# Two more attention units normalised and projected on the chip instead of through DRAM

## The chip, the cores and the metric

The kernel runs on one core of one Trainium2 chip. The metric is the device time of one execution in microseconds (us); lower is better. Times of views of the profile count from the start of the profiled span.

## The reference, cut to what matters

Two residual blocks on x of shape (4, 1024, 256), that is B = 4 sequences of T = 1024 tokens with C = 256 channels, all in float32:

```python
# block 1: causal attention along T, 16 heads of 16 channels, ALiBi bias
qkv = layernorm(x) @ w_attn.T
att = softmax(q @ k.T / 4 + bias)          # per head, keys up to the query
x   = x + (att @ v) @ w_proj.T
# block 2: an encoder layer on layernorm(x): attention among the B = 4 rows at
# each position, layer norm, then one of 8 experts (two linear layers with a
# GELU between) for each token, layer norm; added to x
x   = x + encoder_layer(layernorm(x))
```

The part that the change touches is the end of block 1: dividing `att @ v` by the sums of the softmax (normalising), and multiplying by `w_proj` (projecting) before the sum goes into x.

## The kernel before, in words

**Blocks and units.** T is cut into 8 column blocks of 128 queries. Attention is computed in 20 *units* (list `units`, indices 0 to 19). Units 0 to 11 take one sequence and two column blocks. The last two column blocks, the seventh and the eighth, are taken one at a time: units 12 to 15 are the four sequences of the seventh block, units 16 to 19 the four sequences of the eighth. Unit 15 is "the seventh block's fourth unit", unit 18 "the last unit but one", unit 19 is `last_unit`.

**Positions.** Each unit treats its 16 heads in G = 4 groups of four heads, g0 to g3. The keys of a group are taken in *rounds* of up to 512 columns. Two rounds make one *position* of the main loop; a late unit has two rounds a group, so one position a group. `begins[u]` is the first position of unit u. In this text (18 g2) is the position of unit 18, group 2. A position issues, in this order: the score matmuls `sk` of its first round (`score_next`; TensorE into PSUM, then `exp` on ScalarE into tiles `p`, then a causal mask on GpSimd), an "E slot" (VectorE work), a "D slot" (TensorE work of other stages), the `sk` of its second round, and the matmuls `pv` (probabilities times values, `weigh_next`) of the position before. After `pv`, ScalarE or VectorE moves the result to a tile `yt`. Row 16 of each head's 32 rows in `yt` is the sum of the softmax.

**PSUM.** During attention PSUM is four pairs of banks, `s0` to `s3`, given out strictly in turn (`pair_of_banks`). A round of scores takes two pairs, a `pv` takes one, and work in the D slot takes halves of further pairs (`bank`, which hands out the second half of the last pair first). Whoever asks for a pair waits until the readers of its last contents have finished.

**Way through DRAM (units 0 to 18).** `weigh` stores `yt` to DRAM (`y`). Some us later the planner issues `load_sums` (sums from DRAM, laid out over partitions), `invert` (reciprocal on VectorE, stored to DRAM as `r`), `load_y` (two broadcast loads `su` of `r`, two loads `yc` of y), `divide` (`yc` times `su`, VectorE) and `project` (four rows of matmul `op`, with `wp`, then VectorE adds PSUM to x in `add_attended`). The due times after the unit's last `pv` are the constants `SUMS_BY` to `PROJECTED_BY` (7, 14, 18, 29 and 31 us by the planner's clock).

**Way on the chip (unit 19 alone).** `normalise(g)` multiplies `yt` by the constant matrix `slot_sum` on TensorE, which spreads each head's sum over its 32 rows (`sum`), takes the reciprocal of the 128x128 result on VectorE and multiplies it with `yt` (`yn`). `project_slots` multiplies the four `yn` with `wp_slots`, a copy of `w_proj` in the 32-row layout that `load_slotted` fetches.

**What follows.** Once all four sequences of column block i are in x, a `front(i)` is queued: layer norm, projection `qkvp`, attention among the four rows (`pr`, `sc`, `pv` and `ctx` on VectorE), output projection `ao`, layer norm, routing (`key`, `best`, `hot`, `rank`, `place`). At most two fronts run together, and `E` stages go to VectorE while `D` stages go to a D slot. The fronts share the single tile `qkv`, so one front's `qkvp` copies wait until the front before has read it for the last time. When attention ends, the tail starts: front(7), what is left of front(6), and then the 38 tiles of the experts.

**Order.** All engines run in the order in which this program issues instructions (`manual_schedule`). The order comes from a planner that keeps a clock for TensorE, VectorE and ScalarE (`time`), adds an estimated cost for each step (for a D slot's work, VectorE is charged 0.35 of the stated cost), and takes a stage once its estimated inputs are ready. So a change of one unit's steps also moves other steps from one position to another. Every instruction issued through `Core` has the source line L587; the names of tiles tell the groups apart.

Of the kernel before, what the change touches and what calls it, by code (L numbers as in the profile page):

```python
# [29 lines left out]
F32 = mybir.dt.float32  # L30
# [7 lines left out]
P = 128  # L38
B, T, C = 4, 1024, 256
H, D, E = 16, 16, 8  # L40
S = 32
G = H // 4
NT = T // P
# [3 lines left out]
W = 256  # L47
PC = W // P
NC = T // W
# [22 lines left out]
KQ_BUFS = 2  # L72
# [3 lines left out]
SUMS_BY, INVERTED_BY, Y_BY, DIVIDED_BY, PROJECTED_BY = 7.0, 14.0, 18.0, 29.0, 31.0  # L76
# [529 lines left out]
def fast_layer(ctx: ExitStack, tc: tile.TileContext, odd, x, wq, wk, wv, wp, w_in, w_out, w_r,  # L606
# [32 lines left out]
    fact = ctx.enter_context(pool("fact", 1))  # L639
    ends = ctx.enter_context(pool("ends", 1))  # L640
# [3 lines left out]
    act = attention.enter_context(pool("act", 1))  # L644
# [16 lines left out]
    def pair_of_banks(name):  # L661
        half_of.clear()
        n_pairs[0] += 1
        taken.append(n_pairs[0] % 4)
        return ps_s.tile([P, 2, QC], F32, tag=f"s{n_pairs[0] % 4}", name=name)

    def bank(name):
        if tail_banks:
            return tail_banks[0].tile([P, QC], F32, tag="m", name=name)
        if half_of:  # L670
            return half_of.pop()
        pair = pair_of_banks(name)
        halves[pair.tensor.name] = [], []
        half_of.append(pair[:, 1])
        return pair[:, 0]

    batches = [(c, b) for c in range(NC) for b in range(B)]
# [2 lines left out]
    units = [(n, 0, PC if n < (NC - 1) * B else 1) for n in range(NC * B)]  # L680
    units += [(n, i, 1) for i in range(1, PC) for n in range((NC - 1) * B, NC * B)]
    last_unit = len(units) - 1
    xs = {}

    def load_x(n):
# [161 lines left out]
    sums, at = [], 0  # L847
# [4 lines left out]
    held = {}  # L852
# [187 lines left out]
    def heads_of(n):  # L1040
        return y_of[n].rearrange("g p w -> (g p) w").rearrange("(h s) w -> h s w", s=S)

    def load_sums(u):
        part_of_row = units[u][2] * H
        nc.sync.dma_start(
            sums[u], heads_of(u)[:, D].rearrange("h (k w) -> h k w", w=part_of_row)
        )
# [30 lines left out]
    def add_attended(u, pm):  # L1078
        n, i, size = units[u]
        at = xs[batches[n]][:, i:i + size].rearrange("p n c -> p (n c)")  # L1080
        nc.vector.tensor_tensor(at, at, pm[:, :size * C], ALU.add)

    def project(u):
        yc, _ = held.pop(("y", u))
        pm = bank(f"op_{u}")
        for i in range(units[u][2]):
            for cc in range(CC):
                nc.tensor.matmul(
                    pm[:, i * C:(i + 1) * C], yc[:, cc, i * P:(i + 1) * P], wp_sb[:, cc],
                    start=cc == 0, stop=cc == CC - 1,  # L1090
                )
        add_attended(u, pm)
# [4 lines left out]
    for j in range(4):  # L1097
        at = slice(j * S, (j + 1) * S)
# [11 lines left out]
                )  # L1110
            held["wp"].append(w)

    def normalise(g):
        if g % 2 == 0:
            held["yn", g // 2] = ends.tile([P, 2, W], F32, tag="su", name=f"yn_{g}", bufs=2)
        yt, yn = (held[k, g // 2][:, g % 2, :P] for k in ("yt", "yn"))
        pm = bank(f"sum_{g}")[:, :P]
        nc.tensor.matmul(pm, slot_sum, yt, start=True, stop=True)
        nc.vector.reciprocal(yn, pm)
        nc.vector.tensor_tensor(yn, yn, yt, ALU.mult)  # L1120

    def project_slots():
        pm = bank(f"op_{last_unit}")
        for g in range(G):
            nc.tensor.matmul(
                pm[:, :C], held["yn", g // 2][:, g % 2, :P], held["wp"][g // 2][:, g % 2],
                start=g == 0, stop=g == G - 1,
            )
        add_attended(last_unit, pm)


    def numbered(name, shape, pattern, up=0, base=0, dtype=F32, into=keep):
# [878 lines left out]
    queue, running = [], []  # L2011
# [78 lines left out]
    begins = [0]  # L2090
# [4 lines left out]
    def at_E(k, what, cost=0.0):  # L2095
        of_E.setdefault(k, []).append((cost, what))

    def at_D(k, cost, what):
        of_D.setdefault(k, []).append((cost, what))
# [4 lines left out]
    for u, (n, i, size) in enumerate(units):  # L2104
        c, b = batches[n]
# [17 lines left out]
    due_E, due_D = [], []  # L2123

    def attended(u, at):
        size = units[u][2]
        if u == last_unit:
            return
        for by, what, cost in (
            (SUMS_BY, load_sums, 0.0), (INVERTED_BY, invert, 0.3), (Y_BY, load_y, 0.0),  # L2130
            (DIVIDED_BY, divide, 0.5),
        ):
            due_E.append((at + by, cost, lambda what=what: what(u)))
        due_D.append((at + PROJECTED_BY, 0.9 * size, lambda: projected(u)))

    def projected(u):
        n, i, size = units[u]
        c, b = batches[n]
        project(u)
        if b == B - 1:  # L2140
            queue.extend(front(PC * c + i + k, fact, 1, False) for k in range(size))

    def pop_due(due, now):
        some = sorted((it for it in due if it[0] <= now), key=lambda it: it[0])
# [1 line left out]
            due.remove(it)  # L2146
        return [(cost, what) for _, cost, what in some]

    at_E(2 * begins[last_unit] + 1, load_slotted)
    for g in range(2):  # L2150
        at_D(begins[last_unit] + 2 + g, 0.5, lambda g=g: normalise(g))

    def more_rows():
        nc.vector.tensor_scalar(q_by, q_by, -4.0, at_row, ALU.mult, ALU.add)
# [74 lines left out]
    def weigh_next(some):  # L2229
        taken.clear()  # L2230
        weigh(some)
        end = on_tensor(SWITCH + sum(columns_of(u, r) for u, _, r, _ in some) * COLUMN)
        read_at(busy("ACT", 0.4, end))
        u, g, r, _ = some[-1]
        if g == G - 1 and r == n_rounds(u) - 1:
            attended(u, time["ACT"])
# [27 lines left out]
    for it in running:  # L2264
        it.ready = 0.0
    for g in range(2, G):
        normalise(g)
    load_sums(last_unit)
    project_slots()
    tail = ctx.enter_context(pool("tail", 1))  # L2270
    work = ctx.enter_context(pool("work", 2))
    ps_x = ctx.enter_context(pool("ps_x", 1, space=PSUM))
# [53 lines left out]
    def begin(it):  # L2326
        if it.kind == "DQ" and ("qkv",) in held or it.kind[1:] == "C" and part.placed < NT - 1:
            return 1e9
        return max(it.ready, free[engine_of[it.kind[0]]])
# [26 lines left out]
    while threads:  # L2356
# [4 lines left out]
        at, _, it = min((begin(it) + FIRST_BY * n, n, it) for n, it in enumerate(threads))  # L2361
# [14 lines left out]
    n = 0  # L2376
    while experts.left():
# [4 lines left out]
        if n == 11:  # L2382
            pm = bank("n_badp")
# [4 lines left out]
@with_exitstack  # L2388
def tile_layer(ctx: ExitStack, tc: tile.TileContext, *args):
    nc = tc.nc  # L2390
    flag = ctx.enter_context(tc.tile_pool(name="flag", bufs=1))
    odd = flag.tile([P, 1], I32, tag="odd", name="odd")
    fast_layer(tc, odd, *args)
    again = nc.values_load(
        odd[0:1, 0:1], min_val=0, max_val=1,
        skip_runtime_bounds_check_because="a comparison's result",
    )
    with tc.If(again > 0):
        general_layer(tc, *args)
# [75 lines left out]
```

## Time and profile before

| | |
|---|---|
| three runs | 836.48, 839.2, 842.09 us; median 839.2 us |
| the profiled execution | 839.28 us, of which the span is 837.1 us |
| mean granted TensorE clock | 0.94 |
| busy over the span | TensorE 719.4 us (86%), VectorE 544.6 us (65%), ScalarE 416.6 us (50%), GpSimd 251.1 us (30%) |
| last `pv` of attention starts | 628.07 us |
| last sum of attention into x (unit 19, `x<-op`) | 641.60 us |

The profiled execution lies on the median, 0.08 us from it. The busy shares are means over three stages with different limits: attention up to some 630 us, the two last fronts up to some 700 us, and the experts. In a timeline of one engine each line has the start, the duration, the engine, line and operation, the tiles (out<-in), the shape, the count and, in brackets, the idle time before with the engine and tile that ended it.

### The profile page before, as it was taken

How to read it: one execution, taken by the hardware profiler on the slowest of the kernel's cores; microseconds unless marked ns; L12 is line 12 of the kernel's file. 1: busy time of each engine (PE TensorE's matmuls, PEld its weight loads, DVE VectorE, ACT ScalarE, POOL GpSimd, SP SyncE). 2: the span in 40 equal slices, each digit the busy share in tenths (PEclk: the TensorE clock that was granted, in tenths of full speed). 3: DMA queues.
4: the chain of work that ended last, by engine and by line, in shares of the span. 5: the costliest groups of instructions: out<-in, count | busy, mean ns of one | idle time of the engine just before them, and what ended most of it. 6: DMA issues, size and time to landing. Idle time of an engine off the chain costs nothing. (4 is left out here: it accounts for less than half of the span.)

```text
span 837.1 us, 22503 instructions
## 1 busy us (share of the span) xinstructions
PE 719.4 (86%) x8917; PEld 540.2 (65%) x8917; DVE 544.6 (65%) x1316; ACT 416.6 (50%) x625; POOL 251.1 (30%) x360
## 2 busy tenths in 40 slices
PE   4988879995999999998989999999983689678982
PEld 2766657674666756665667767787762368567772
DVE  7337224546678877946964739487695869884663
ACT  1455436563647556735654658578460235323540
POOL 5534102211113221102211212122130235637885
PEclk9799889998999999998999999999997699978997
DMA  7454444424344324333354635445315512333430
GB/s 215 117 148 137 143 134 134 144 63 123 94 119 129 108 77 147 98 104 95 93 142 141 185 109 144 123 126 158 94 53 195 177 37 90 93 97 120 124 103 24
DMA packets 75219, 99.56 MB, mean 119 GB/s; under 512 B 19496, under 2 KB 58723, under 8 KB 74596
## 3 DMA queue, kind: packets, MB, share of 16 engines
q1 hardware_dynamic: 64576, 79.63, 32.1%
q0 software_dynamic: 4864, 14.16, 5.6%
q10 hardware_dynamic: 5668, 4.25, 1.7%
q8 instruction: 73, 1.20, 0.6%
q14 instruction: 38, 0.31, 0.1%
HBM read 61.55 MB, written 35.12 MB: 115 GB/s over the span
## 5 line engine op out<-in xcount | busy, mean ns | idle before, releaser
L587 ACT ACTIVATE p<-sk 128x1024 f32<-128x1024 f32 (+1 forms) x320 | 287.0, 939 | 162.8 <-PE sk L587 147.8
L986 POOL TENSOR_SCALAR_AFFINE_SELECT p<-p 128x512 f32<-128x512 f32 (+1 forms) x160 | 103.6, 651 | 397.8 <-ACT p L587 395.9
L587 PE MATMUL sk<-slots 32*128 32x128 f32 (+1 forms) x3456 | 181.7, 328 | 21.2 <-DVE kq L587 10.0
L587 PEld LDWEIGHTS sk<-slots 32*128 32x128 f32 x3456 | 138.1, 188 | 64.9 <-issue 26.8
L587 PE MATMUL pv<-p,v 128*32 128x128 f32 (+1 forms) x3456 | 144.5, 314 | 10.4 <-ACT p L587 4.6
L587 PEld LDWEIGHTS pv<-p,v 128*32 128x32 f32 x3456 | 96.7, 111 | 48.3 <-issue 8.3
L587 PE MATMUL qkvp<-w_in,ut 128*128 128x264 f32 (+1 forms) x224 | 79.1, 489 | 0.0
L587 PEld LDWEIGHTS qkvp<-w_in,ut 128*128 128x128 f32 x224 | 40.3, 194 | 26.7 <-issue 22.4
L587 PE MATMUL oe<-w,ge 128*128 (+1 forms) x152 | 45.2, 423 | 12.9 <-DVE given L587 4.5
L587 PE MATMUL qkp<-xt,wqk 128*128 128x256 f32 x208 | 54.4, 407 | 0.2 <-ACT p L587 0.2
L1813 POOL DMA_INDIRECT given<-rows,rows x38 | 43.2, 1137 | 27.6 <-DVE at_t L587 11.6
L587 PE MATMUL hid<-mt,w 128*128 128x128 f32 x304 | 47.0, 293 | 0.5 <-ACT ge L587 0.5
L587 PEld LDWEIGHTS qkp<-xt,wqk 128*128 128x128 f32 x208 | 39.6, 200 | 11.1 <-issue 3.3
L587 ACT COPY qkv<-qkvp 128x512 f32<-128x512 f32 (+1 forms) x28 | 15.3, 555 | 58.5 <-PE qkvp L587 43.9
L587 PEld LDWEIGHTS hid<-mt,w 128*128 128x128 f32 x304 | 41.9, 200 | 2.0 <-ACT ge L587 1.0
L587 DVE COPY qkv<-qkvp 128x264 f32<-128x264 f32 x28 | 11.9, 431 | 46.9 <-PE qkvp L587 46.8
L1929 POOL DMA_INDIRECT out_dram<-o,out_rows x38 | 38.9, 1024 | 8.8 <-issue 6.3
L587 DVE TENSOR_REDUCE sc<-pr 128x64 f32<-128x1024 f32 x32 | 39.0, 1220 | 1.1
L587 PEld LDWEIGHTS oe<-w,ge 128*128 128x128 f32 x152 | 28.0, 205 | 17.8 <-DVE given L587 5.7
L587 DVE TENSOR_TENSOR pv<-qkv,sc 128x1024 f32<-128x1024 f32 x32 | 39.2, 1224 | 0.4 <-issue 0.3
L587 DVE TENSOR_TENSOR pr<-qkv 128x1024 f32<-128x1024 f32 x32 | 39.2, 1226 | 0.0
L587 PE MATMUL vp<-wv,xt 128*128 128x256 f32 x128 | 35.3, 423 | 0.0
(333 smaller groups left out, 1040.2 us busy)
## 6 DMA issues: line engine op xcount, KB each, us to landing
slots<-k SPq DMA_DIRECT2D x128, 80.0 KB
k<-kq SPq DMA_DIRECT2D x32, 256.0 KB
v<-v SPq DMA_DIRECT2D x16, 288.0 KB
v<-v SPq DMA_DIRECT2D x4, 1152.0 KB
x<-in_x_dram SPq DMA_DIRECT2D x16, 256.0 KB
y<-yt SPq DMA_DIRECT2D x16, 256.0 KB
rows<-x SPq DMA_DIRECT2D x32, 128.0 KB
slots<-k SPq DMA_DIRECT2D x64, 64.0 KB
```

What stands on the lines that cost most here:

```text
L587: ins = made(*args, **kwargs)
L986: nc.gpsimd.affine_select(blocks, blocks, pattern=[[0, 2], [0, size], [1, P]], compare_op=ALU.is_ge, fill=0.0, base=0, channel_multiplier=-1,)
L1813: nc.gpsimd.indirect_dma_start(out=self.hx, out_offset=None, in_=t.rows_of, in_offset=bass.IndirectOffsetOnAxis(ap=t.rows_[:, self.j:self. ...
L1929: ins = nc.gpsimd.indirect_dma_start(out=out.rearrange("t n c -> (t n) c"), out_offset=bass.IndirectOffsetOnAxis(ap=t.table.out_rows[:, t. ...
```

## The change

Unit 15 and unit 18 go the way that unit 19 goes. Step by step:

- `on_chip = (15, 18, 19)`. For 15 and 18, `attended` issues only `load_sums` (the sums are still wanted for a later check), and no `invert`, `load_y`, `divide` or `project`.
- For each of the two, `normalise(u, g)` is put into the D slots of positions `begins[u] + 2 + g`, g = 0 to 3, and `project_slots(u)` into that of `begins[u] + 6`. The next unit begins at `begins[u] + 4`, so the last two sums and the projection stand in the positions g0 to g2 of the following unit.
- `load_slotted` moves from the start of unit 19 to the start of unit 14.
- The tiles `yn` of units 15 and 18 are taken from the buffers of `kq`, the second `yn` tile of unit 19 from those of `yc`.
- A front is queued when all four of its units are projected, counted in `n_projected`, and no longer by the index of the sequence.

```diff
+    on_chip = ((NC * B - 1), last_unit - 1, last_unit)
...
-    def normalise(g):
+    def normalise(u, g):
         if g % 2 == 0:
-            held["yn", g // 2] = ends.tile([P, 2, W], F32, tag="su", name=f"yn_{g}", bufs=2)
-        yt, yn = (held[k, g // 2][:, g % 2, :P] for k in ("yt", "yn"))
-        pm = bank(f"sum_{g}")[:, :P]
+            held["yn", u, g // 2] = (
+                ends.tile([P, 2, W], F32, tag="yc" if g else "su", name=f"yn_{u}_{g}", bufs=2)
+                if u == last_unit else
+                act.tile([P, 2, W], F32, tag=f"kq{g // 2}", name=f"yn_{u}_{g}", bufs=KQ_BUFS)
+            )
+        yt, yn = (held[k][:, g % 2, :P] for k in (("yt", g // 2), ("yn", u, g // 2)))
+        pm = bank(f"sum_{u}_{g}")[:, :P]
         nc.tensor.matmul(pm, slot_sum, yt, start=True, stop=True)
         nc.vector.reciprocal(yn, pm)
         nc.vector.tensor_tensor(yn, yn, yt, ALU.mult)
 
-    def project_slots():
-        pm = bank(f"op_{last_unit}")
+    def project_slots(u):
+        pm = bank(f"op_{u}")
         for g in range(G):
             nc.tensor.matmul(
-                pm[:, :C], held["yn", g // 2][:, g % 2, :P], held["wp"][g // 2][:, g % 2],
+                pm[:, :C], held["yn", u, g // 2][:, g % 2, :P], held["wp"][g // 2][:, g % 2],
                 start=g == 0, stop=g == G - 1,
             )
-        add_attended(last_unit, pm)
+        add_attended(u, pm)
...
     def attended(u, at):
         size = units[u][2]
-        if u == last_unit:
+        if u in on_chip:
+            if u < last_unit:
+                due_E.append((at + SUMS_BY, 0.0, lambda: load_sums(u)))
             return
...
+    n_projected = [0] * NT
+
     def projected(u):
         n, i, size = units[u]
-        c, b = batches[n]
-        project(u)
-        if b == B - 1:
-            queue.extend(front(PC * c + i + k, fact, 1, False) for k in range(size))
+        c = batches[n][0]
+        (project_slots if u in on_chip else project)(u)
+        for k in range(PC * c + i, PC * c + i + size):
+            n_projected[k] += 1
+            if n_projected[k] == B:
+                queue.append(front(k, fact, 1, False))
...
-    at_E(2 * begins[last_unit] + 1, load_slotted)
-    for g in range(2):
-        at_D(begins[last_unit] + 2 + g, 0.5, lambda g=g: normalise(g))
+    at_E(2 * begins[on_chip[0] - 1], load_slotted)
+    for u in on_chip:
+        for g in range(2 if u == last_unit else G):
+            at_D(begins[u] + 2 + g, 0.5, lambda u=u, g=g: normalise(u, g))
+        if u < last_unit:
+            at_D(begins[u] + 2 + G, 1.8, lambda u=u: projected(u))
...
     for g in range(2, G):
-        normalise(g)
+        normalise(last_unit, g)
     load_sums(last_unit)
-    project_slots()
+    project_slots(last_unit)
```

## The prediction

> **What bounds the kernel now.** I read the page first, then the table by stages around the end of attention, then the timelines of VectorE and TensorE there.
>
> The page's busy line says TensorE over the whole span, which hides that the stages differ:
>
> ```profile
> PE 719.4 (86%) x8917; PEld 540.2 (65%) x8917; DVE 544.6 (65%) x1316; ACT 416.6 (50%) x625; POOL 251.1 (30%) x360
> ```
>
> By stages (columns: stretch, length, busy us and instructions of PE, PEld, DVE, ACT, POOL, granted clock, DMA share, GB/s):
>
> ```profile
> 520.00:560.00 40.00, 39.72 (x752) 30.73 (x752) 26.30 (x55) 24.32 (x33) 7.84 (x13) 1.00 0.38 111
> 560.00:590.00 30.00, 27.79 (x690) 23.84 (x690) 22.45 (x49) 23.02 (x29) 6.01 (x11) 1.00 0.57 163
> 590.00:630.00 40.00, 35.97 (x726) 27.52 (x718) 31.41 (x73) 21.06 (x27) 9.62 (x13) 1.00 0.21 62
> 630.00:642.00 12.00, 5.77 (x20) 4.43 (x16) 3.60 (x8) 0.27 (x1) 0.00 (x0) 0.72 0.66 221
> 642.00:665.00 23.00, 9.08 (x45) 4.88 (x45) 21.83 (x61) 4.11 (x8) 5.49 (x5) 0.69 0.48 160
> ```
>
> The reader should see three limits in turn. To 590, TensorE is full. From 630 to 642 nothing is: VectorE 3.60 and TensorE 5.77 of 12 us. From 642 to 665 VectorE is full, 21.83 of 23. VectorE's timeline names the hole:
>
> ```profile
> 629.12 0.25 DVE L587 RECIPROCAL inverse<-sums 128x16 f32<-128x16 f32 x1
> 635.29 0.43 DVE L587 TENSOR_TENSOR yc<-yc,su 128x256 f32<-128x256 f32 x1 [5.92 <-DMA yc<-y]
> 637.97 0.42 DVE L587 TENSOR_TENSOR x<-x,op 128x256 f32<-128x256 f32 x1 [2.25 <-PE op L587]
> 638.33 0.96 DVE L587 RECIPROCAL yn<-sum 128x128 f32<-128x128 f32 x1
> 641.60 0.42 DVE L587 TENSOR_TENSOR x<-x,op 128x256 f32<-128x256 f32 x1 [0.79 <-PE op L587]
> 641.94 0.35 DVE L587 TENSOR_TENSOR own<-low_con,expert 128x192 f32<-128x192 f32 x1
> ```
>
> Unit 18 goes through DRAM after attention has ended; unit 19's last sums stand behind it on TensorE and VectorE. I take the start of `own`, 641.94, as the mark: from there VectorE has no gap to 665, and the order of instructions from there on is the same in the changed program on PE, DVE and ACT. Whatever moves `own` moves the end.
>
> For attention's price per position I use the starts of `pv`:
>
> ```profile
> 547.39 1.96 PE L587 MATMUL pv<-p,v 128*32 128x128 f32 x64
> 551.62 1.95 PE L587 MATMUL pv<-p,v 128*32 128x128 f32 x64 [0.28 <-ACT p L587]
> 554.61 1.13 PE L587 MATMUL op<-wp,yc 128*128 128x256 f32 x4
> 556.94 1.95 PE L587 MATMUL pv<-p,v 128*32 128x128 f32 x64
> ...
> 617.95 1.95 PE L587 MATMUL pv<-p,v 128*32 128x128 f32 x64
> 620.93 0.49 PE L587 MATMUL sum<-yt,slot_sum 128*128 128x128 f32 x2
> 623.26 1.96 PE L587 MATMUL pv<-p,v 128*32 128x128 f32 x64
> 628.07 1.96 PE L587 MATMUL pv<-p,v 128*32 128x128 f32 x64 [2.85 <-DVE count L587]
> ```
>
> A position with an empty D slot takes 4.23 us (547.39 to 551.62); with one `op`, 5.32; with one `sum` (next instruction 0.33 later), also 5.31. So I price a D slot at 1.09 us or its TensorE time, whichever is more. The last line matters most: the last `pv` waits 2.85 us for a bank that VectorE, late, has yet to read (`count`).
>
> **What the Trainium skill says.** "PSUM — Partial Sum Buffer", section "Engine vs sequencer instructions": VectorE's queue is strictly first in, first out, and matmuls start in program order. The trace agrees: unit 19's `sum` and `yn` stand behind unit 18's wait. [...] Here `inverse` at 629.12 needs a store and a load in series before `yc` at 635.29, 6.2 us for both with their issue[...]. "VectorE: DVE Perf Modes", section "First, the fixed hardware budget": the reciprocal is an iterated divide. The trace agrees: 951 ns for `yn<-sum` 128x128 against 292 for the product of that size.
>
> **Removed after attention.** Unit 18's waits and steps, 629.12 to 638.33 on VectorE. The next limit is the last `yt` copy (ends 630.36) and its `sum`; with these at 631, unit 19's last sums would end with `own` at about 634.6. Taken alone: 641.94 - 634.6 = 7.3 us gained. Per unit three VectorE pieces (0.25 + 0.43, the sum into x stays) and five DMAs on SP's queue go too. I cost SP at 0: nothing waited on it there except `yc`.
>
> **Added on TensorE in attention**, in positions from the instruction order of the changed program:
> - Unit 15: three `sum` alone in empty slots, (15 g2), (15 g3), (16 g0): unit 15, with 7 key blocks, pays 0.91 for a small D slot (`pv` at 500.37, 505.29 and 509.30: 4.92 with one `op`, 4.01 empty), so 0.91 + 0.91 + 1.0 = 2.8. The fourth beside `qkvp`: 0.32. Projection has 8 matmul passes for 4: `op` of unit 15 costs 2.0 at (16 g2), and 1.09 goes at (17 g1). `op` of unit 14 moves from (16 g3) to (16 g2): 0. Sum +4.0.
> - Unit 18 up to the end of the D slot of (19 g0): `sum` and `utp` join `ctp` at (18 g2), 2.36 for 1.09, +1.27. At (18 g3) `sum`, `op` of unit 16, `ao` and one `qkvp`, 8.1 for 4.94, +3.16. At (19 g0) 8.48 for 9.08, -0.6. Sum +3.8. The last `qkvp` of front(6), before at (19 g1), is now in (19 g0).
> - Waits for banks held by a late VectorE, found by walking both queues: the first `sum` of unit 15 comes at 508.4 but VectorE is in `pr`/`sc` to 511.2 (0.9 us); `rank` (0.3 more than its 0.73 now); `utp` behind `u` (0.6). Sum +1.8, an estimate from below 0 to 4: a different interleaving may lose nothing.
>
> The D slot of (19 g0) ended at 602.98; now at 602.98 + 4.0 + 3.8 + 1.8 = 612.6.
>
> **Added on VectorE, where I think it decides.** Eight `yn` pairs of 1.26 us (616.98 to 618.24) = 10.1, less 2 x 0.68. The planner charged 0.18 each, so it does not see the delay. In the changed order, all this stands behind the last `qkv` copy, which now waits for TensorE at 612.6 + 0.6 = 613.2 (spacings measured in the old timeline): `u` 1.30, `key` 0.78, `yc` 0.35, `best` to `equal` 1.45, told 0.15, `equal` to `hot` 2.37, `yn` 1.26, `x` 0.35, `u<-rows` 2.40, `pr`/`sc` 2.39, `x` 0.36, `yn` 1.26, `rank` to `at_place` 3.36, three `pr`/`sc` 7.2, `yn` 1.26. Sum 26.2, so `count` comes at 639.4 against 627.86. TensorE wants that bank at about 633.6 (its 625.2, + 4.0 + 1.8, and + 2.3 for unit 18 with (19 g1) 2.94 shorter and (19 g2) 1.44 longer, plus 0.3): it waits some 6 us instead of 2.85. Last `pv` 639.6 to 641.6, `sum` to 641.8, first `yn` at 642.1, and from `yn` to `own` 3.6 us as now (638.33 to 641.94): `own` at 645.7. That is 3.8 us later; with 0.2 us for the pieces I rounded, 4.0.
>
> Covered at nothing: the earlier `load_slotted` (two GpSimd memsets of 0.5 us, 8 DMAs of 0.45 us on SP) lies beside GpSimd's idle time and ahead of slot fills needed a unit later; if not covered, up to 3.6 us. The experts' weights, issued at 634.10 now, start some 9 us later, but their first copy is at 693.23.
>
> Sum on the profiled execution: 839.28 + 4.0 = 843.3 us; it lies on the median, so that is the forecast for it too, +0.5%. A measurement here tells about 1% from no change.
>
> **Rivals.**
> A. *The removed wait wins.* If VectorE does the 26.2 us list in under 20, TensorE decides the end: last `pv` at 633.6, `own` at 639.7, -2.2 us, 837; without the bank waits (1.8) and with lone sums at their own 0.32 (2.0), 833. All of the 7.3 would be 832. For it: VectorE idles some 15 us between 585 and 613 waiting for `qkvp`. Against: its order puts the list behind those copies.
> B. *Slower by over 1%: banks pinned by VectorE.* Eight `sum` banks are each freed only by a reciprocal queued behind front work; a wait of one `pr` and `sc` (2.4 us) at three of them beyond the 1.8 above gives +7.2, 850. It decides from two such waits, 848. For: VectorE is busy 18.29 of 20 us at 500 to 520. Against: TensorE comes back to the same pair only some 3.5 us later.
> C. *Nothing moves*: the 4.0 and errors of the walk cancel, 839. Counted in the forecast's own range.
>
> **How the numbers follow.** Forecast with C (838 to 847.7): 0.52. A: 0.28, of which 0.12 under 830.9 (gains in the order that I don't see). B: 0.20. So faster by over 1% 0.12, within 1% 0.68, slower 0.20. The range 831 to 851 leaves out A's far part (0.12) and that of B (some 0.08).
>
> **What would show it.** Right: `inverse` and its 5.92 us gone after 629; the last `pv` waits about 6 us for `count` near 639; `own` near 646; `pv` periods with a lone `sum` near 5.3. Wrong: no wait for `count` and `own` before 640 (A), or waits of `sk` or `pv` for `yn` over 1 us in units 15 to 19 (B). A changed duration from 642 on in the tail would break the mark.

## The result, and the profile after

The changed kernel takes 841.5 us (median of 20 executions, 838.26 to 846.82), beside 836.4 us for the kernel before on the same chip (833.48 to 843.03): ratio 1.0055, 95% interval 1.0037 to 1.0073. It is 0.55% slower, and the interval leaves out 1. The profiled execution took 843.85 us, its span is 842.1 us, the mean granted clock 0.94. In the traces the end of attention, from the last `pv` to unit 19's sum into x, became 6.2 us shorter, and 12 to 13 us were paid before it (the table by cuts below).

The busy line of the page:

```profile
PE 722.7 (86%) x8941; PEld 542.8 (64%) x8941; DVE 552.2 (66%) x1328; ACT 416.9 (49%) x625; POOL 253.4 (30%) x360
```

The table by stages (stretch, length, busy us and instructions of PE, PEld, DVE, ACT, POOL, granted clock, DMA share, GB/s):

```profile
590.00:630.00 40.00, 36.14 (x577) 27.27 (x581) 25.85 (x70) 18.78 (x24) 4.87 (x9) 1.00 0.22 62
630.00:642.00 12.00, 6.69 (x167) 5.75 (x164) 10.75 (x14) 4.20 (x6) 3.00 (x3) 0.88 0.05 13
642.00:665.00 23.00, 12.17 (x87) 7.05 (x79) 19.13 (x55) 3.93 (x8) 4.89 (x5) 0.77 0.56 191
```

Where no engine was full before (630 to 642, VectorE 3.60 us), VectorE is now full with 10.75 of 12 us. In 590 to 630 it is less busy than before (31.41 us): its work has moved back. VectorE's timeline shows what it is full of:

```profile
613.04 0.43 DVE L587 COPY qkv<-qkvp 128x264 f32<-128x264 f32 x1 [2.29 <-PE qkvp L587]
...
637.34 1.22 DVE L587 TENSOR_REDUCE sc<-pr 128x64 f32<-128x1024 f32 x1
638.48 0.95 DVE L587 RECIPROCAL yn<-sum 128x128 f32<-128x128 f32 x1
639.53 0.29 DVE L587 TENSOR_TENSOR yn<-yn,yt 128x128 f32<-128x128 f32 x1
639.74 0.16 DVE L587 TENSOR_SCALAR count<-sum 128x8 f32<-128x8 f32 x1
...
647.31 0.42 DVE L587 TENSOR_TENSOR x<-x,op 128x256 f32<-128x256 f32 x1 [0.79 <-PE op L587]
647.65 0.35 DVE L587 TENSOR_TENSOR own<-low_con,expert 128x192 f32<-128x192 f32 x1
```

From the last `qkv` copy to `count` VectorE works for 26.7 us without a wait. TensorE's timeline shows who waits for that, and two waits earlier on:

```profile
592.48 1.13 PE L587 MATMUL sum<-wp,yc 128*128 128x256 f32 x4 [2.17 <-DVE yc L587]
...
614.03 1.96 PE L587 MATMUL pv<-p,v 128*32 128x128 f32 x64
...
627.70 1.95 PE L587 MATMUL pv<-p,v 128*32 128x128 f32 x64 [1.45 <-DVE yn L587]
...
633.02 1.95 PE L587 MATMUL pv<-p,v 128*32 128x128 f32 x64
639.96 3.17 PE L587 MATMUL pv<-p,v 128*32 128x128 f32 x64 [4.99 <-DVE count L587]
```

The last `pv` waits 4.99 us (2.85 before), and then takes 3.17 us instead of 1.96. The first line is the projection of unit 16 at (18 g3): it takes the second half of a pair of banks, which is handed out under the name of the `sum` before it.

To compare kernels I cut each trace at five places that all orders share, and name a `pv` by the position in which it is issued. A: from the start of `pv` in (15 g0) to that of `pv` in (18 g0). B: to `pv` in (19 g0). C: to the last `pv`. D: to unit 19's sum into x. E: to the end of the span. The rows below the first two are the experiments of the next section. Each ratio compares with executions of the kernel before on the same chip, while the stages are those of one profiled execution each.

| us | A | B | C | D | E | from the first cut | ratio to before (95%) |
|---|---|---|---|---|---|---|---|
| before | 70.9 | 32.8 | 24.0 | 13.5 | 195.5 | 336.7 | |
| after | 76.5 | 38.4 | 25.9 | 7.4 | 194.8 | 342.9 | 1.0055 (1.0037 to 1.0073) |
| norecip | 76.5 | 37.9 | 22.9 | 6.2 | 194.8 | 338.2 | 1.0000 (0.9974 to 1.0026) |
| only15 | 77.3 | 36.7 | 22.0 | 14.8 | 203.1 | 353.9 | 1.0189 (1.0153 to 1.0224) |
| only18 | 72.9 | 33.8 | 25.7 | 6.1 | 195.3 | 333.8 | 0.9981 (0.9960 to 1.0003) |
| sooner18 | 72.1 | 32.4 | 24.0 | 7.2 | 194.0 | 329.7 | 0.9916 (0.9882 to 0.9949) |
| loadearly | 71.7 | 32.8 | 24.0 | 14.0 | 193.4 | 335.9 | 1.0000 (0.9982 to 1.0018) |
| latepr | 71.0 | 32.9 | 21.6 | 7.2 | 203.2 | 335.9 | 0.9970 (0.9954 to 0.9987) |
| only15s | 75.6 | 41.6 | 22.1 | 8.6 | 202.5 | 350.4 | 1.0134 (1.0096 to 1.0173) |
| sooner1518 | 79.0 | 38.7 | 22.1 | 8.8 | 201.3 | 350.0 | 1.0115 (1.0068 to 1.0161) |
| pair15 | 75.0 | 37.9 | 25.9 | 7.5 | 194.8 | 341.2 | 1.0041 (1.0021 to 1.0061) |
| sooner16 | 76.5 | 40.0 | 25.9 | 8.1 | 192.8 | 343.4 | 1.0043 (1.0023 to 1.0063) |
| mended | 76.6 | 37.7 | 25.9 | 7.7 | 195.7 | 343.5 | 1.0014 (0.9998 to 1.0031) |

Five of these (before, only18, sooner18, loadearly, latepr) have the same order on TensorE through A: 70.9 to 72.9. So a difference under some 2 us in A says nothing, while C repeats to 0.01 us in before, sooner18 and loadearly (24.0) and in after, pair15, sooner16 and mended (25.9). In E there are two main orders, each the same on TensorE, VectorE, ScalarE and GpSimd: eight kernels with that of before take 192.8 to 195.6 us, and the four of only15, latepr, only15s and sooner1518 take 201.3 to 203.2. only18 has one of its own (195.3).

### The profile page after: what moved, and what is told of

Same layout as the page of the kernel before. It is cut to its first block, busy times and chain, and to the rows that moved or that the text cites. A ratio compares the mean times of both kernels' runs of the same rounds, so it can differ in the third digit from the quotient of the medians.

```text
span 842.1 us, 22549 instructions
## 1 busy us (share of the span) xinstructions
PE 722.7 (86%) x8941; PEld 542.8 (64%) x8941; DVE 552.2 (66%) x1328; ACT 416.9 (49%) x625; POOL 253.4 (30%) x360
## 5 line engine op out<-in xcount | busy, mean ns | idle before, releaser
L988 POOL TENSOR_SCALAR_AFFINE_SELECT p<-p 128x512 f32<-128x512 f32 (+1 forms) x160 | 105.4, 662 | 407.8 <-ACT p L587 405.6
L587 PE MATMUL sk<-slots 32*128 32x128 f32 (+1 forms) x3456 | 183.4, 329 | 22.9 <-DVE kq L587 9.1
```

What stands on the lines that cost most here:

```text
L587: ins = made(*args, **kwargs)
L988: nc.gpsimd.affine_select(blocks, blocks, pattern=[[0, 2], [0, size], [1, P]], compare_op=ALU.is_ge, fill=0.0, base=0, channel_multiplier=-1,)
```

## The experiments

My theory after the result: the DRAM wait of unit 18 (D) is gone, and is paid back by TensorE's added work in A and B and by VectorE's list behind the last `qkv` copy in C. By VectorE's list I mean all that stands in its order from there to `count`.

**norecip: VectorE's list without the reciprocals.**

```diff
-        nc.vector.reciprocal(yn, pm)
-        nc.vector.tensor_tensor(yn, yn, yt, ALU.mult)
+        nc.vector.tensor_tensor(yn, pm, yt, ALU.mult)
```

> The changed kernel without the reciprocals in the twelve normalisations of units 15, 18 and 19: yn is sum times yt, so the division of these three units is left out of the result, and VectorE has 0.95 us less in each; the order on all other engines is the same. My theory: three of them stand between the last qkv copy and count, so count moves from 639.7 to about 636.9; two more stand in the chain from the last pv to own; own at about 642 to 643 for 647.65, and the time 4.5 to 5.5 us under the changed kernel, so at or just under the kernel before (ratio 0.999 to 1.001). Rival 'TensorE's added work alone sets the price and the wait for count costs nothing': only the two in the last chain count, 1.9 us under the changed kernel, ratio 1.003.

Measured: 836.83 us, ratio 1.0000. VectorE's timeline of this kernel:

```profile
611.32 0.43 DVE L587 COPY qkv<-qkvp 128x264 f32<-128x264 f32 x1 [2.29 <-PE qkvp L587]
...
618.02 0.28 DVE L587 TENSOR_TENSOR yn<-sum,yt 128x128 f32<-128x128 f32 x1
...
635.04 0.15 DVE L587 TENSOR_SCALAR count<-sum 128x8 f32<-128x8 f32 x1
```

From the copy to `count` it is 23.72 us instead of 26.70: three times 0.95 less, and 2.9 us on the list are worth 3.0 us in C (25.9 to 22.9). In A and B, where TensorE is full, seven reciprocals less are worth 0 and 0.5 us. In D 0.7 of the 1.2 us gained are the last `pv`, which took 2.47 us here instead of 3.17, which leaves 0.5 for the two reciprocals there. So VectorE's list decides in C, and the rival (the wait for `count` costs nothing) falls.

**only15 and only18: one unit alone.**

```diff
-    on_chip = ((NC * B - 1), last_unit - 1, last_unit)
+    on_chip = ((NC * B - 1), last_unit)           # only15
+    on_chip = (last_unit - 1, last_unit)          # only18
```

> The changed kernel with unit 15 on the chip and unit 18 again through DRAM. My theory (the removed DRAM wait of unit 18 is paid back by added TensorE work in attention and by VectorE's list behind the last qkv copy): unit 15's +4.0 us of TensorE work and some 1 us of bank waits are paid, and the 5.9 us wait for yc of unit 18 stays after attention, so own starts at about 646 to 648 and the time is 4 to 6 us above the kernel before (ratio 1.005 to 1.007). Rival 'the price comes from unit 18 alone': within 1 us of the kernel before. Rival 'unit 15 gains because its four small loads leave the queues': 1 to 2 us under it.

> The changed kernel with unit 18 on the chip and unit 15 again through DRAM. My theory: no unit 15 cost (4 to 5 us less than the changed kernel), unit 18's +3.8 us on TensorE are paid, the DRAM wait of 7.3 us is gone, and count comes at about 631 to 635 since the last qkv copy is at 609 and some of front(6) now stands behind count; own at about 637 to 641, the time 1 to 4 us under the kernel before (ratio 0.995 to 0.999). Rival 'the price comes from unit 18': as slow as the changed kernel, ratio 1.005 or more. Rival 'the removed wait is all there is': 7 us under, ratio 0.991.

Measured: only15 853.09 us, ratio 1.0189, far above all I expected; only18 834.29 us, ratio 0.9981, within what I expected, though its interval just includes no change, and by another way: `count` came at 619.97 us and not at 631 to 635. The two parts don't add: +1.89% and -0.19%, but +0.55% together. The table says why. only18 is 7.4 us shorter in D and pays 1.1 us in B (against the mean of the other four of its order in A) and 1.7 in C, where TensorE waits for `yn` (1.87 and 0.88 us) and no longer for `count`. That its A is the longest of the five is no price of the change: the order is the same, and 1.1 us of it are one stall inside a `pv` (1.40 us, 0.34 in before) for which the profile names no cause. only15 pays A and most of B as the changed kernel does, keeps the wait in D, and has 7.6 us more in E, where nothing of unit 15 stands. VectorE's timeline past the mark `own`, first of before and then of only15:

```profile
643.21 0.57 DVE L587 TENSOR_REDUCE top<-sc 128x64 f32<-128x256 f32 x1
...
648.54 0.57 DVE L587 TENSOR_REDUCE tot<-sc 128x64 f32<-128x256 f32 x1
```

```profile
648.51 0.35 DVE L587 TENSOR_TENSOR own<-low_con,expert 128x192 f32<-128x192 f32 x1
...
651.02 1.22 DVE L587 TENSOR_REDUCE sc<-pr 128x64 f32<-128x1024 f32 x1
...
656.54 0.57 DVE L587 TENSOR_REDUCE top<-sc 128x64 f32<-128x256 f32 x1
...
661.08 0.58 DVE L587 TENSOR_REDUCE tot<-sc 128x64 f32<-128x256 f32 x1 [2.11 <-ACT sc L587]
```

In this kernel the planner put one `pr` and `sc` of front(6) behind `own`. `top`, which needs all four `sc`, comes 8.0 us after `own`, where before it is 1.3 us (643.21 after 641.94), and `tot` 12.6 us after it instead of 6.6.

**latepr: that push by itself.** sooner18 (below) with

```diff
+        if p == len(rounds) // 2 - 2:
+            time["DVE"] += 2.0
```

> The kernel before with unit 18's due times halved and the planner's VectorE clock put 2 us later at the last position but one: one pr and sc of front(6) is pushed from before count into the tail, behind own, and the tail's order follows; attention is unchanged. My theory (this push is what made the tail of the kernel with unit 15 alone 7.6 us longer): count and own come some 2 us earlier, own to the end takes 201 to 203 us instead of 193.7, net 5 us slower than with unit 18's due times halved alone, ratio 0.997 to 0.999. Rival 'the tail was longer for another reason (DMA, front(7))': 193 to 195 us from own to the end and a gain of 2 us, ratio 0.989.

Measured: 834.46 us, ratio 0.9970, 0.54% above sooner18. C is 2.4 us shorter (the pair is no longer ahead of `count`) and E 9.2 us longer. Its VectorE timeline repeats that of only15 (the line number is one higher by an added constant):

```profile
631.53 0.35 DVE L588 TENSOR_TENSOR own<-low_con,expert 128x192 f32<-128x192 f32 x1
...
634.05 1.22 DVE L588 TENSOR_REDUCE sc<-pr 128x64 f32<-128x1024 f32 x1
...
639.56 0.57 DVE L588 TENSOR_REDUCE top<-sc 128x64 f32<-128x256 f32 x1
...
644.11 0.58 DVE L588 TENSOR_REDUCE tot<-sc 128x64 f32<-128x256 f32 x1 [2.11 <-ACT sc L588]
```

TensorE, VectorE, ScalarE and GpSimd have only15's order through E, and E is as long (203.2 and 203.1 us). So 2.4 us of VectorE work that falls out of attention cost 9.2 us in the tail. How much of this is the later chain of front(6) (`sc`, `top`, `tot`) and how much the order of the experts, which changed with it, isn't shown. The changed kernel has all four pairs ahead of `count`, so it doesn't pay this. Why the planner keeps the pair in with both units and not with unit 15 alone I didn't trace.

**sooner18: the hole removed without the change.** The kernel before with

```diff
+SOONER = 0.5
...
-            due_E.append((at + by, cost, lambda what=what: what(u)))
-        due_D.append((at + PROJECTED_BY, 0.9 * size, lambda: projected(u)))
+            sooner = SOONER if u == last_unit - 1 else 1.0
+            due_E.append((at + sooner * by, cost, lambda what=what: what(u)))
+        sooner = SOONER if u == last_unit - 1 else 1.0
+        due_D.append((at + sooner * PROJECTED_BY, 0.9 * size, lambda: projected(u)))
```

> The kernel before with the planner's due times of unit 18 alone halved (sums, reciprocal, loads, division, projection all sooner after its last pv); the only move in the order is that unit 18's inverse comes ahead of the first yn of unit 19, at about 617 instead of 629.1, with its loads behind it. My theory: unit 18's waits of 5.9 us leave the end of attention without any work added to attention; yc is there by about 623, the next limit is the last yt and its sum at 631, own at about 635.5 for 641.94, the time 5 to 7 us under the kernel before (ratio 0.992 to 0.994). Rival 'the last pv and count are then late for another reason': 0 to 2 us under. Rival 'the loads wait in the queue however early they are issued': no change.

Measured: 829.01 us, ratio 0.9916: 7.0 us under the kernel before by the ratio, and faster than both kernels. Its VectorE timeline:

```profile
612.83 0.24 DVE L588 RECIPROCAL inverse<-sums 128x16 f32<-128x16 f32 x1
...
623.71 0.16 DVE L588 TENSOR_SCALAR count<-sum 128x8 f32<-128x8 f32 x1
...
627.50 0.42 DVE L588 TENSOR_TENSOR x<-x,op 128x256 f32<-128x256 f32 x1 [2.01 <-PE op L588]
...
631.43 0.35 DVE L588 TENSOR_TENSOR own<-low_con,expert 128x192 f32<-128x192 f32 x1
```

`inverse` stands 10.9 us ahead of `count` instead of 1.3 us behind it; the loads behind it land meanwhile, D falls from 13.5 to 7.2 us, and A, B and C stay within what one order spreads. It is the only instruction that VectorE and TensorE have in another place. So the hole came from where one 0.24 us instruction stood in the order, not from the way through DRAM.

**loadearly: the moved `load_slotted` alone.** The kernel before with

```diff
-    at_E(2 * begins[last_unit] + 1, load_slotted)
+    at_E(2 * begins[NC * B - 2], load_slotted)
```

> The kernel before with load_slotted alone moved from the start of unit 19 to the start of unit 14, as the change does; nothing else moves on TensorE, VectorE or ScalarE. My prediction costed this at nothing: within 0.2% of the kernel before. Rival: GpSimd's two memsets and SP's eight issues delay the slot fills and scores of units 14 and 15, up to 3.6 us slower, ratio 1.004.

Measured: 836.44 us, ratio 1.0000 (0.9982 to 1.0018). What I costed at nothing costs nothing, to 0.2%.

**pair15: two D slots less.**

```diff
-            at_D(begins[u] + 2 + g, 0.5, lambda u=u, g=g: normalise(u, g))
+            at_D(begins[u] + 2 + (g if u > NC * B - 1 else g + 1 - g % 2), 0.5,
+                 lambda u=u, g=g: normalise(u, g))
```

> The changed kernel with unit 15's sums in pairs: g0 and g1 both in (15 g3), g2 and g3 both in (16 g1), so that (15 g2) and (16 g0) have an empty D slot again; the same work, two D slots less, and apart from the order of two qkvp nothing else moves. My theory (a D slot has a fixed price of about 0.9 to 1.0 us there, and TensorE's delay carries through VectorE's list to the end): 1.91 us saved and 0.32 paid at (16 g1), so 1.6 us under the changed kernel, ratio 1.0035 to the kernel before. Rival 'a sum costs its own 0.32 us wherever it stands': no change, 1.0055. Rival 'pairs pin the banks until VectorE comes to them': 1 to 2 us slower than the changed kernel, 1.007.

Measured: 841.46 us, ratio 1.0041. The interval holds both 1.0035 and 1.0055, so the ratio leaves it open. In the trace A is 1.45 us shorter, B 0.5, and C unchanged, 1.8 us in all from the first cut, close to the 1.6 expected; but 2 us in A is the spread of one order. It leans to a fixed price for a D slot and doesn't show it.

**sooner16 and mended: unit 16's wait at (18 g3).** Due times of unit 16 times 0.9 in the changed kernel; mended has this and pair15.

> The changed kernel with the due times of unit 16 shortened by a tenth: the only move in the order is that unit 16's inverse comes ahead of one pv, its two sums and the statistics of front(5), some 4 us earlier. My theory (the 2.17 us that TensorE waits at (18 g3) for unit 16's yc is part of the change's price, and TensorE's delay carries through the last qkv copy and VectorE's list to the end): that wait falls under 0.3 us, count and own come 1.9 to 2.2 us earlier relative to unit 15, ratio 1.003 to the kernel before. Rival 'another wait takes its place at (18 g3)': the wait moves to another tile and nothing is gained, ratio 1.0055.

> The changed kernel with both repairs: unit 15's sums in pairs and unit 16's inverse 4 us earlier. My theory: the two gains add since both shorten TensorE's way to the last qkv copy, 1.6 + 2.0 us, ratio 1.001 to the kernel before; VectorE's list behind that copy is untouched and still makes the last pv wait 4 to 5 us. Rival 'VectorE's queue from 580 on sets the pace whatever TensorE does': the last pv's wait grows by what TensorE gains, ratio 1.0055 as the changed kernel.

Measured: sooner16 840.91 us, ratio 1.0043 (1.0023 to 1.0063); mended 838.55 us, ratio 1.0014 (0.9998 to 1.0031). The mechanism expected of sooner16 didn't come: `inverse` was earlier, but TensorE still waited 1.79 us for `yc`, and 1.00 us in mended. (In sooner16 the matmuls behind that wait then ran slowly, and B grew by 1.6 us; see the last section.) SP's queue in mended shows why:

```profile
573.29 0.35 SPq L1056 DMA_DIRECT2D r<-inverse  x1
577.36 0.38 SPq L1039 DMA_DIRECT2D y<-yt  x1
577.83 3.19 SPq L942 DMA_DIRECT2D slots<-k  x4
581.11 0.37 SPq L926 DMA_DIRECT2D v<-v  x1
581.57 0.62 SPq L1071 DMA_DIRECT2D su<-r  x1
```

The store of `r` is issued at 573.29, but the load `su` stands behind a store that waits 3.6 us for a `yt`, four slot fills and the 1152 KB load of `v`, until 581.57. So the store is 5.3 us earlier than in the changed kernel (578.59), and the load only 1.6 (583.17). With both repairs the kernel's interval lies below that of the changed one (1.0031 against 1.0037), so by the ratios some 0.4 of the 0.55% can be bought back. Where this was gained isn't shown: the profiled execution of mended took 843.15 us, 4.6 us over its own median, and from the first cut it is no shorter (343.5 us against 342.9).

**only15s and sooner1518: two that missed.** only15s is only15 with unit 18's due times halved; sooner1518 is sooner18 with unit 15's halved too.

> Unit 15 on the chip, unit 18 through DRAM but with unit 18's due times halved: the only difference from the kernel with unit 15 alone is that unit 18's inverse stands ahead of two pr and sc, some 7 us earlier. It removes the wait for yc after attention (6.7 us) from that kernel. My theory: the wait goes, own starts some 7 us earlier, and the longer time from own to the end (202.8 us against 195.2 before, since one pr and sc of front(6) was pushed behind own) stays: 8 to 9 us less than with unit 15 alone, ratio 1.008 to 1.010. Rival 'the longer tail came from the wait too': 15 us less, ratio 1.000. Rival 'another limit takes the wait's place': 0 to 3 us less, ratio 1.015 or more.

> The kernel before with the due times of units 15 and 18 halved, all units but 19 through DRAM: front(6) is queued and its qkvp matmuls are issued about a position earlier, as the change does, but without the change's sums and doubled projection on TensorE. My theory (VectorE's list behind the last qkv copy sets the end of attention): that copy comes some 4 us earlier, count 1 to 4 us earlier, ratio 0.987 to 0.991 against 0.9916 with unit 18 alone. Rival 'the earlier front takes TensorE time from attention at no gain': 0.992 or more. Rival 'the tail's order pays it back': 1.0.

Measured: only15s 848.99 us, ratio 1.0134, some 4.6 us under only15 by the ratios where I expected 8 to 9. D fell by 6.2 us as expected and E stayed at 202.5; but B grew by 4.9 us. TensorE's order in A and B is the same as in only15, and its timeline shows where they come from:

```profile
589.17 2.05 PE L588 MATMUL op<-wp,yc 128*128 128x256 f32 x4 [3.26 <-DVE yc L588]
591.00 1.97 PE L588 MATMUL op<-w_out,ct 128*128 128x264 f32 x4
```

This is unit 16's projection again. The wait was 3.26 us (1.82 in only15), and after it the matmuls ran at half speed (2.05 us instead of 1.10) for 5.8 us, in which they did what took 2.9 in only15: together 4.3 of the 4.9 us.

sooner1518 took 848.38 us, ratio 1.0115, where I expected 0.987 to 0.991. It had two faults that hide what an earlier front(6) is worth: `inverse` of a unit came so early that VectorE waited 7.58 us for its sums at 537.27, and again one `pr` and `sc` fell behind `own` (E 201.3). It shows only that sooner isn't better in itself.

## Why the prediction was right

It said 843.3 us, 4.0 us or 0.5% above the kernel before. The medians lie 5.1 us apart, 0.55% by the ratio, and the profiled execution took 843.85 us. The size and the mechanism were right, but that the absolute times agree so closely is in part luck. The forecast stood on 839.2 us for a kernel that ran at 836.4 here; and the profiled execution reached the first cut 1.2 us earlier than that of before (499.21 against 500.37), where TensorE, VectorE and ScalarE have the same order. From the first cut the change costs 6.2 us in the traces, and the prediction's own steps (`own` at 645.7) come to 3.8:

- *Unit 15 on TensorE, +4.0 and 0.9 of waits:* A is 4.7 us above the mean of the five kernels with the old order (71.7). The first late bank cost 0.64 us (0.9 predicted), and the wait for `p` behind it was 0.61 (0.31 before).
- *Unit 18 up to (19 g0), +3.8 and 0.9 of waits:* B is 5.6 us longer. The waits predicted for `rank` (0.3 more) and for `utp` (0.6) didn't come; that for `rank` was 0.28 in all against 0.73 before. In their place TensorE waited 2.17 us at (18 g3) for unit 16's `yc`, the one wait there that the walk missed.
- *Last `qkv` copy:* predicted 613.2, measured 613.04, which is 1.0 us later than predicted when both are counted from the first cut. *The list behind it:* 26.2 us predicted, 26.7 measured, with `count` at 639.74. norecip shows that this list sets the time of the last `pv`.
- *Last `pv`:* predicted at 639.6 after a wait of some 6 us; measured 639.96 after 4.99. Its length was wrong: I took 1.96 us, it took 3.17. This mis-sized term and the later start of `sum` behind it put `own` at 647.65 instead of 645.7.
- *The tail:* taken as unchanged, it gave back 0.7 us (E, 195.5 to 194.8), within what that order differs by.
- *`load_slotted` at nothing:* held, by loadearly.
- *The way out of DRAM, 7.3 us:* right in size. D fell by 6.2 us with the slow `pv` inside it, by 7.4 in only18, and sooner18 gained 7.0.

Rival A fell because the list took 26.7 us, not under 20. What was said for it was also misread: between 585 and 613 us VectorE idles 10.2 us in before, not some 15, and 6.3 of these wait for `qkvp`. Rival B had one wait of its kind, 1.45 us for `yn` at (19 g2) and 0.64 in unit 15: under the two full waits of 2.4 us from which it would have decided. By the prediction's own sign (such a wait over 1 us) the first counts for B; but it lies in C, where VectorE works through its list without a gap, and so costs nothing. A price of B's size exists, but by another way: in only15, sooner1518 and latepr one `pr` and `sc` of front(6) falls out of attention, and the tail is 6 to 9 us longer. The prediction had read from the changed kernel's order of instructions that its tail keeps the old order; in the other it would have lost some 7 us more, an estimate from these E.

## What to carry to other kernels

Before you move work to get rid of a wait on DRAM, look at where the first instruction of that chain stands in the order: here moving one 0.24 us reciprocal, with the loads behind it, from behind `count` to 10.9 us ahead of it gave 0.8%, while taking the chain away and paying for it on TensorE and VectorE lost 0.55%. Walk every engine's queue behind the last result that it waits for, instruction by instruction: that list (26.7 us), not the busy shares, gave the end of attention. Where a planner makes the order, a part of a change can't be priced by itself: compare whole orders, and look for stages that fall out of the stretch in which they were covered.

## What the hardware did that I had not expected

- A wait on TensorE can cost more than its length. After 4.99 us the last `pv` took 3.17 us for 1.96, after 3.65 us (norecip) 2.47, after 3.26 us (only15s) a projection 2.05 for 1.10; after 2.85 us nothing was lost in before and sooner18, but loadearly's took 2.53 after 2.86. It isn't the length alone: after 1.79 us (sooner16) the projection took 2.08 us, and after 2.17 us (after) its full-speed 1.13. The granted clock goes with it: it is 0.50 from 640 to 642 us in after and from 595 to 597 in sooner16, but 1.00 from 628 to 630 in before and from 624 to 626 in sooner18. The Trainium skill, "TensorE: Matmul & The Clock Gate", section "What's actually happening", says that the clock is halved after an idle window of about 3.4 us that runs free of the kernel. The long waits agree. If that window is the 3.4 us before the clock falls, it need not be wholly idle here: in sooner16 TensorE was busy for 1.78 us of them (591.03 to 594.44). That waits of 1.8 to 2.9 us go both ways would fit a window that runs free and weighs how busy TensorE was, which no run here tests by itself.
- The product of a PSUM tile and an SBUF tile, 128x128, takes 0.28 us (norecip), as much as between two SBUF tiles (0.29), while the reciprocal of that PSUM tile takes 0.95. So it is the reciprocal itself, not the read from PSUM, that makes the normalisation costly.
